# A preact convolution on one core: a regular pattern of combined images, all sums on the scalar engine, and a new order of its and the Pool's work

## The chip, the cores and the metric

The kernel runs on one core of a Trainium2 chip. The metric is the device time in microseconds (us) of one execution. The engines are PE (matmuls), PEld (its weight loads), DVE (vector), ACT (scalar), POOL (GpSimd) and SP (sync, which issues loads and stores).

## The reference

160 images of 128 channels and 32x32 pixels. Each gets a group norm (32 groups of 4 channels), then a 3x3 convolution with one of five weight sets, quantised in two steps, and is added to its input.

```python
x, U: (160, 128, 32, 32), (5, 128*128*9)      # both float32
s1 = (U.max() - U.min()) / 3;  v1 = s1 * floor(U / s1)
s2 = s1 / 5;                   v2 = s2 * floor((U - v1) / s2)
w  = (v1 + v2).reshape(640, 128, 3, 3)
y  = conv2d(group_norm(x, groups=32, eps=1e-5).reshape(32, 640, 32, 32),
            w, padding=1, groups=5)
return x + y.reshape(x.shape)
```

## The kernel before

The matmuls run in fp16. To keep the precision, the normalised image is split into a high part (a cast to fp16) and a low part (the difference). Pairs of rows share products: sums and differences of neighbouring rows go into a pair tile `m`, the rest goes directly into `eo`, and `m` is added to `eo` in between. There are two kinds of image from image 14 on:

- A **direct** image D: ACT makes `z` (normalised, f32) and casts it to `hi`; DVE makes `lo = z - hi` and the row combinations of `lo` alone. PE uses plain taps on `hi` and combinations of `lo`.
- A **combined** image C: the row differences and sums are taken of the raw image in f32 (`v`), ACT scales and casts them (`vh`), DVE makes the low part (`vl`). PE needs fewer matmuls. The first and the last row of the differences touch the padding; these two rows of 32 values are made by the Pool.

```python
STEADY = 14                      # images 14 to 155 may be combined
COMBINED = (1, 4, 6)             # residues modulo 8 of the combined images
MEASURED = (1, 5)                # residues measured by DVE, the others by ACT

def combine(self, i):
    v = self.v[i] = self.wide.tile([P, 2048], F32, ...)
    nc.gpsimd.tensor_scalar(v[:, :W], x[:, W:2*W], minus, -1.0, ALU.add, ALU.mult)
    nc.gpsimd.tensor_scalar(v[:, last:H*W], x[:, last-W:last], minus, 1.0, ALU.add, ALU.mult)
    nc.vector.tensor_sub(v[:, W:last], x[:, :last-W], x[:, 2*W:])
    # ... and two more DVE instructions for the sums and differences of pairs
```

One iteration of the main loop, cut to its order. Each engine works off its own instructions in this program order. `measure(k, (0,))` is the sum over an image and `(1,)` the sum of squares about the mean, each one ACT pass; `residual` evacuates `eo` to `sum`; `accumulate` has the Pool issue the DMA that adds `sum` to the image; `leave` copies half of `m` out of the matmul memory; `pairs` adds `m` to `eo` on DVE. The matmuls, `conv(i)`, come first: the pair sums of image i+1, then the rest of image i.

```python
self.residual(j); self.accumulate(j)                       # ACT, POOL
if self.combined(i + 1): measure stage 0                   # ACT
self.leave(i + 1)                                          # ACT
if not self.combined(i + 1): measure stage 0               # ACT
if self.combined(i + 3): self.high_combined(i + 3)         # ACT: vh
else:                    self.normalise(i + 3)             # ACT: z
measure stage 1                                            # ACT
if not self.combined(i + 3): self.high_part(i + 3)         # ACT: hi
# ... every 8 images: deviation, scales, deviations        # ACT, POOL
# ... 12 times: keep_column (a column of new weights)      # ACT, POOL
low_combined(i + 2)  or  low_part(i + 2)                   # DVE: vl / lo
take(later, 1)                                             # DVE: weight step
combinations(i + 2)  if direct                             # DVE
self.pairs(i + 1)                                          # DVE
if self.combined(i + 4): self.combine(i + 4)               # POOL rows, DVE
# ... images of residues 1 and 5 measured on DVE
```

## Time and profile before

| before | |
|---|---|
| time, median of 3 runs | 1057.66 us (1057.18 to 1061.2) |
| span in the profile | 1054.1 us |
| busy: PE, DVE, ACT, POOL | 94, 86, 80, 34% |
| combined images (`vh`) | 53 |
| images measured on DVE | 38 |

The prediction below shows the lines of the page, the waits and the chain.

A second measure is my own count from the trace and is called **lost** below: the time from each matmul's start to the next one's, less the median of that distance for its shape, summed over all distances that are more than 0.1 us too long.

### The profile page before, as it was taken

Reading aid. Unit: us, or ns where it says so; the run is one execution under the profiler, and the core shown is the slowest. Engines: PE = TensorE matmul, PEld = TensorE weight load, DVE = VectorE, ACT = ScalarE, POOL = GpSimd, SP = SyncE. Lnnn points to the kernel's source line nnn. Section 1 sums busy time; section 2 is a strip of 40 time slices with the busy share of each in tenths; the row PEclk is TensorE's granted clock in tenths of the full one; section 3 lists DMA queues with packets and bytes.
Section 4 is the critical chain, followed back from the end, with each engine's and each line's share of the span. In section 5 each row is a group of like instructions: output and inputs, shape, how many; then the busy total and the mean of one; then the engine's idle time right before and its main releaser. Section 6 shows DMA issues by size and latency. Waiting matters only on the chain.

```text
span 1054.1 us, 15898 instructions
## 1 busy us (share of the span) xinstructions
PE 990.0 (94%) x5910; PEld 574.7 (55%) x5910; DVE 909.0 (86%) x1387; ACT 845.4 (80%) x1145; POOL 363.4 (34%) x519
## 2 busy tenths in 40 slices
PE   1889999999999999999999999999999999999997
PEld 0335555555555555555556565555555655555554
DVE  7978898988999999889999988898998888888763
ACT  4889888888888887878888888888887888887660
POOL 3514244343425152523343333415161613233310
PEclk9999999999999999999999999999999999999999
DMA  9537989999999989899899999999989899987763
GB/s 364 209 100 219 247 235 248 249 248 265 264 258 251 260 235 270 234 277 269 231 276 240 264 245 254 276 254 249 261 242 247 231 265 261 266 236 182 175 174 125
DMA packets 67287, 254.42 MB, mean 241 GB/s; under 512 B 5248, under 2 KB 5248, under 8 KB 67200
## 3 DMA queue, kind: packets, MB, share of 16 engines
q1 hardware_dynamic: 45168, 173.09, 48.1%
q0 software_dynamic: 22032, 80.23, 39.6%
q8 instruction: 48, 0.79, 0.3%
q14 instruction: 39, 0.32, 0.1%
HBM read 89.19 MB, written 83.89 MB: 164 GB/s over the span
## 4 chain that ended last, share of the span: by engine, by line
PE 69%; DVE 21%; ACT 6%; issue 3%; DMA 1%; POOL 0%; SPq 0%; DVEq 0%; ACTq 0%
PE eo L608 32%; PE m L634 20%; PE eo L634 15%; DVE lo L568 4%; DVE eo L697 2%; DVE rows L582 2%; DVE eo L696 2%; ACT junk L192 2%; ACT z L511 2%; DVE v L544 2%; ACT hi L519 1%; DVE rows L584 1%; DVE rows L585 1%; DVE v L547 1%; DVE v L550 1%
## 5 line engine op out<-in xcount | busy, mean ns | idle before, releaser
L634 PEld LDWEIGHTS <-wt 128*128 128x128 f16 x3780 | 367.8, 98 | 255.5 <-DVE eo L697 36.8
L608 PE MATMUL eo<-hi,wt 128*128 128x496 f16 (+1 forms) x1908 | 458.7, 377 | 1.1 <-ACT wt L476 1.1
L724 POOL DMA_DIRECT2D xt<-sum x153 | 134.8, 881 | 478.1 <-ACT sum L711 473.2
L608 PEld LDWEIGHTS <-wt 128*128 128x128 f16 x1980 | 194.6, 100 | 186.5 <-issue 4.2
L711 ACT ACTIVATE sum<-eo 128x1024 f32<-128x1024 f32 x153 | 156.2, 1021 | 97.1 <-PE eo L634 88.4
L634 PE MATMUL eo<-rows,wt 128*128 128x248 f16 (+1 forms) x1248 | 187.9, 273 | 0.0
L634 PE MATMUL m<-rows,wt 128*128 128x496 f16 (+1 forms) x624 | 153.6, 383 | 27.9 <-DVE eo L697 27.8
L568 DVE TENSOR_TENSOR lo<-z,hi 128x1024 f16<-128x1024 f32 x107 | 130.9, 1224 | 55.3 <-ACT hi L519 55.3
L561 DVE SCALAR_TENSOR_TENSOR vl<-v,rstd,vh 128x2048 f16<-128x2048 f32 x53 | 124.4, 2347 | 22.8 <-ACT vh L555 22.8
L199 ACT ACTIVATE junk<-xt,mv 128x1024 f16<-128x1024 f32 x122 | 139.2, 1141 | 0.3
L192 ACT ACTIVATE junk<-xt 128x1024 f16<-128x1024 f32 x122 | 129.4, 1061 | 11.5 <-DMA xt<-in_x_dram 11.3
L696 DVE TENSOR_TENSOR eo<-m,m 128x512 f32<-128x512 f32 x157 | 108.9, 693 | 29.0 <-ACT m L687 27.0
L511 ACT ACTIVATE z<-xt,shift,rstd 128x1024 f32<-128x1024 f32 x107 | 132.9, 1242 | 0.6 <-POOL shift L242 0.6
L687 ACT COPY m<-m 128x512 f32<-128x512 f32 x157 | 91.6, 584 | 49.6 <-PE m L634 49.6
L555 ACT ACTIVATE vh<-v,rstd 128x2048 f16<-128x2048 f32 x53 | 105.9, 1998 | 22.6 <-POOL v L541 20.0
L634 PE MATMUL eo<-vh,wt 128*128 128x248 f16 (+1 forms) x636 | 121.7, 273 | 0.0
L634 PE MATMUL eo<-vl,wt 128*128 128x248 f16 (+1 forms) x636 | 121.7, 273 | 0.0
L634 PE MATMUL m<-vh,wt 128*128 128x496 f16 (+1 forms) x318 | 120.8, 380 | 0.9 <-DVE eo L697 0.9
L634 PE MATMUL m<-vl,wt 128*128 128x496 f16 (+1 forms) x318 | 120.7, 380 | 0.0
L697 DVE TENSOR_TENSOR eo<-m,m 128x512 f32<-128x512 f32 x157 | 109.8, 700 | 5.4
L519 ACT CAST hi<-z 128x1024 f16<-128x1024 f32 x107 | 111.1, 1039 | 0.9
L582 DVE TENSOR_TENSOR rows<-lo 128x1024 f16<-128x1024 f16 x104 | 72.8, 700 | 1.3
(109 smaller groups left out, 825.5 us busy)
## 6 DMA issues: line engine op xcount, KB each, us to landing
xt<-in_x_dram SPq DMA_DIRECT2D x78, 1024.0 KB, 9.6
out_dram<-xt SPq DMA_DIRECT2D x78, 1024.0 KB, 5.7
xt<-sum POOLq DMA_DIRECT2D x153, 512.0 KB, 7.2
range<-in_L_conv_U_dram SPq DMA_DIRECT2D x4, 576.0 KB, 7.4
u<-in_L_conv_U_dram SPq DMA_DIRECT2D x4, 576.0 KB, 11.8
xt<-in_x_dram SPq DMA_DIRECT2D x4, 512.0 KB, 10.3
out_dram<-xt SPq DMA_DIRECT2D x3, 512.0 KB, 2.9
u<-in_L_conv_U_dram SPq DMA_DIRECT2D x2, 288.0 KB, 3.1
```

What stands on the lines that cost most here:

```text
L192: self.nc.scalar.activation(junk, image, ACTF.Copy, scale=-1.0 / image.shape[1], accum_out=self.mv[:, j, 0:1],)
L199: self.nc.scalar.activation(junk, image, ACTF.Square, bias=self.mv[:, j, 0:1], accum_out=self.mv[:, j, 1:2],)
L511: nc.scalar.activation(z, self.image(i), ACTF.Identity, bias=st.shift[:, j : j + 1], scale=st.rstd[:, j : j + 1],)
L519: self.nc.scalar.copy(hi.rearrange("p h w -> p (h w)"), self.z[i])
L561: self.nc.vector.scalar_tensor_tensor(vl, self.v[i], st.rstd[:, j], self.hi[i], ALU.mult, ALU.subtract)
L568: self.nc.vector.tensor_sub(lo[:, 1 : self.H + 1, :].rearrange("p h w -> p (h w)"), self.z.pop(i), self.hi[i].rearrange("p h w -> p (h w)"),)
L608: nc.tensor.matmul(target[:, h, r0 - h0 : r1 - h0, c0:c1], self.wts[n, col][:, k, :], tile[:, s0 : s0 + r1 - r0, c0 + dw : c1 + dw], start ...
L634: self.nc.tensor.matmul(target[:, :, c0:c1], self.wts[n, col][:, kind, :], source[:, :, c0 + dw : c1 + dw], start=start, stop=stop, skip_g ...
L696: nc.vector.tensor_add(rows[:, :, 0], m[:, 0], m2)
L697: nc.vector.tensor_sub(rows[:, :, 1], m[:, 0], m2)
L711: nc.scalar.mul(self.sum[i], eo, 0.5)
L724: self.nc.gpsimd.dma_start(self.image(i), self.sum.pop(i), accum_op=ALU.add)
```

## The change

It means to let PE run without a gap: fewer matmuls (every second image combined, in place of three of eight), in a regular alternation of C and D. DVE is relieved of its measuring to pay for this, ACT takes it over, and ACT's order is rearranged so that the sums run ahead of the evacuation, and `hi` directly behind `z`. The two rows on the Pool are issued right behind the accumulating DMA. The last image is finished one half (one bank of the matmul memory) at a time.

```diff
-    COMBINED = (1, 4, 6)
-    MEASURED = (1, 5)
+    COMBINED = (1, 3, 5, 7)
+    MEASURED = ()
@@
-    def combine(self, i):
+    def outer_rows(self, i):
         # ... the two gpsimd.tensor_scalar
+    def combine(self, i):
         # ... the three DVE instructions
@@ conv
+        for halves in ((0,), (1,)) if i == self.imgs - 1 else ((0, 1),):
+            for col in self.COLS:
+                if col != self.COLS[0]:
+                    on_the_way(col)
+                self.rest_of_column(i, col, halves)
@@ the loop, in its new order (start-up cases cut)
+            if self.combined(i + 2):
+                self.low_combined(i + 2)
+            if direct:
+                self.low_part(i + 2)
+            take(later, 1)
+            if direct:
+                self.combinations(i + 2)
+            for k in by_scalar:
+                self.measure(k, (0,))
             if i > self.FIRST and not self.by_hand(j):
                 self.residual(j)
                 self.accumulate(j)
+            if self.combined(i + 4):
+                self.outer_rows(i + 4)
             if self.FIRST < i + 1 < self.imgs:
                 self.leave(i + 1)
             if self.combined(i + 3):
                 self.high_combined(i + 3)
             elif self.FIRST < i + 3 < self.imgs:
                 self.normalise(i + 3)
+                self.high_part(i + 3)
             for k in by_scalar:
                 self.measure(k, (1,))
-            if part and not self.combined(i + 3):
-                self.high_part(i + 3)
             # ... deviation, scales, deviations, keep_column as before
             # ... pairs and combine as before
```

More of the change, by code (lines that the diff above doesn't have):

```diff
@@ L543, in combine @@
         )
+    def combine(self, i):
+        nc, H, W = self.nc, self.H, self.W
+        st, j = self.column_of(i)
+        v, x, last = self.v[i], self.image(i), (H - 1) * W
         nc.vector.tensor_sub(v[:, W:last], x[:, : last - W], x[:, 2 * W :])
@@ L592, in halves, with taps @@
         )
-    def taps(self, i, part, col, target, last):
+    def taps(self, i, part, col, target, last, halves=(0, 1)):
         nc, H, W = self.nc, self.H, self.W
@@ L602, in taps @@
         for k in (1, 0, 2):
-            for h in range(2):
+            for h in halves:
                 h0 = h * (H // 2)
@@ L664, in conv, with rest_of_column @@
             self.sums_of_pairs(i + 1)
-        eo = self.eo[i]
-        for col in self.COLS:
-            if col != self.COLS[0]:
-                on_the_way(col)
-            last = col == self.COLS[-1]
-            if not self.combined(i):
-                self.taps(i, (self.hi[i], 0), col, eo, False)
-            for a, kind in enumerate((0, self.MINUS_G2)):
-                both = self.both(i)
-                for j, (d, _) in enumerate(both):
-                    for h in range(2):
-                        rows = slice(h * 16 + a, h * 16 + 16, 2)
-                        to = eo[:, h].rearrange("p (i a) w -> p a i w", a=2)[:, a]
-                        self.product(
-                            to, i, kind, d[:, rows, :], col, False,
-                            last and a == 1 and j == len(both) - 1,
-                        )
-        del self.v[i]
+        for halves in ((0,), (1,)) if i == self.imgs - 1 else ((0, 1),):
[3 more added lines that the diff above has]
+                self.rest_of_column(i, col, halves)
+        del self.v[i]
+    def rest_of_column(self, i, col, halves):
+        eo, both = self.eo[i], self.both(i)
+        if not self.combined(i):
+            self.taps(i, (self.hi[i], 0), col, eo, False, halves)
+        for a, kind in enumerate((0, self.MINUS_G2)):
+            for j, (d, _) in enumerate(both):
+                for h in halves:
+                    rows = slice(h * 16 + a, h * 16 + 16, 2)
+                    to = eo[:, h].rearrange("p (i a) w -> p a i w", a=2)[:, a]
+                    self.product(
+                        to, i, kind, d[:, rows, :], col, False,
+                        col == self.COLS[-1] and a == 1 and j == len(both) - 1,
+                    )
     def leave(self, i):
@@ L887, in run @@
             by_scalar = [k for k in to_measure if not self.by_vector(k)]
-            if i != self.FIRST:
+            direct = self.FIRST < i + 2 < self.imgs and not self.combined(i + 2)
+            if i < self.FIRST:
+                self.residual(j)
+                if i == self.FIRST - 1:
+                    self.leave(i + 1)
+                    self.pairs(i + 1)
+            if self.combined(i + 2):
[5 more added lines that the diff above has]
+                self.combinations(i + 2)
+            if i > self.FIRST and self.by_hand(j):
+                self.residual(j)
+            for k in by_scalar:
+                self.measure(k, (0,))
+            if i > self.FIRST and not self.by_hand(j):
                 self.residual(j)
                 self.accumulate(j)
-            if self.combined(i + 1):
-                for k in by_scalar:
-                    self.measure(k, (0,))
-            if self.FIRST <= i + 1 < self.imgs:
+            if self.combined(i + 4):
+                self.outer_rows(i + 4)
+            if self.FIRST < i + 1 < self.imgs:
                 self.leave(i + 1)
-            if not self.combined(i + 1):
-                for k in by_scalar:
-                    self.measure(k, (0,))
-            part = self.FIRST < i + 3 < self.imgs
             if self.combined(i + 3):
                 self.high_combined(i + 3)
-            elif part:
+            elif self.FIRST < i + 3 < self.imgs:
                 self.normalise(i + 3)
+                self.high_part(i + 3)
             for k in by_scalar:
                 self.measure(k, (1,))
-            if part and not self.combined(i + 3):
-                self.high_part(i + 3)
             for st in middle:
@@ L917, in run @@
             turned = []
-            low = i + 2 if self.FIRST < i + 2 < self.imgs and not self.combined(i + 2) else None
-            if self.combined(i + 2):
-                self.low_combined(i + 2)
-            if low is not None:
-                self.low_part(low)
-            take(later, 1)
-            if low is not None:
-                self.combinations(low)
-            if self.FIRST <= i + 1 < self.imgs:
+            if self.FIRST < i + 1 < self.imgs:
                 self.pairs(i + 1)
```

## The prediction

> **What bounds the kernel now.** I read the page's first part, then the waits of PE, then the chain in one period of eight images (508.10 to 557.84 us), then the timeline of the scalar engine there.
>
> ```profile
> PE 990.0 (94%) x5910; PEld 574.7 (55%) x5910; DVE 909.0 (86%) x1387; ACT 845.4 (80%) x1145; POOL 363.4 (34%) x519
> ...
> q1 hardware_dynamic: 45168, 173.09, 48.1%
> q0 software_dynamic: 22032, 80.23, 39.6%
> ```
>
> PE is the fullest engine, but DVE, ACT and the DMA engines (48.1 + 39.6 = 88%) are not far behind. The waits of all engines hold this line for PE:
>
> ```profile
> PE m L634 <- DVE eo L697: 28.7, 21, 5.2
> ```
>
> One of the 21 is the 5.2 us at 59 to 65 us, where the first direct images end. The other 20, together 23.5 us, lie between 140 and 1000 us, mostly one or two in a period. PE then waits for the DVE to empty the one pair tile `m`. The chain shows what the matmuls cost:
>
> ```profile
> 508.10 1.30 PE m L634 x6
> 509.39 2.63 PE eo L634 x24
> ...
> 518.58 2.59 PE m L634 x12
> ...
> 545.00 1.27 PE eo L608 x6
> 546.27 0.44 PE eo L634 x4
> ```
>
> A direct image D is six pair sums (1.30) and three columns of 1.27 + 0.44, so 6.43 us. A combined image C is 2.59 + 2.63 = 5.22 us. The period holds 5 D and 3 C: 32.15 + 15.66 = 47.8, and 0.4 for the statistics' and weights' small matmuls, 48.2 us. It took 49.74. The rest is waiting, of which the largest piece, in the timeline, is
>
> ```profile
> 543.53 1.47 PE L634 MATMUL m<-rows,wt 128*128 128x512 f16 x6 [1.20 <-DVE eo L697]
> ```
>
> Followed back in the chain it is a run of DVE work without a gap from 532.80, which began late because the cast to `hi` on ACT was late: ACT had done its evacuation, sum, normalisation and second measuring pass first. So **PE bounds each stage, and a queue of ACT then DVE steals about 1.4 us a period from it**.
>
> ACT in order, from the same timeline:
>
> ```profile
> 510.96 1.99 ACT L555 ACTIVATE vh<-v,rstd 128x2048 f16<-128x2048 f32 x1
> 512.86 1.14 ACT L199 ACTIVATE junk<-xt,mv 128x1024 f16<-128x1024 f32 x1
> 513.99 1.00 ACT L711 ACTIVATE sum<-eo 128x1024 f32<-128x1024 f32 x1
> 514.89 0.57 ACT L687 COPY m<-m 128x512 f32<-128x512 f32 x1
> 515.36 1.07 ACT L192 ACTIVATE junk<-xt 128x1024 f16<-128x1024 f32 x1
> 516.41 1.24 ACT L511 ACTIVATE z<-xt,shift,rstd 128x1024 f32<-128x1024 f32 x1
> 517.54 1.14 ACT L199 ACTIVATE junk<-xt,mv 128x1024 f16<-128x1024 f32 x1
> 518.67 1.04 ACT L519 CAST hi<-z 128x1024 f16<-128x1024 f32 x1
> 519.61 0.16 ACT L217 COPY ngm<-pg 128x8 f32<-128x8 f32 x1
> ```
>
> The reader should take start to start, not the durations: vh 1.90, second measuring pass 1.13, evacuation 0.90, `m` copy 0.47, first pass 1.05, z 1.13, hi 0.94. Over the whole period the windows view gives
>
> ```profile
> 508.10:557.84 49.74, 48.54 (x296) 28.51 (x295) 46.02 (x72) 42.29 (x57) 18.28 (x26) 1.00 0.93 250
> ```
>
> (PE, weight loads, DVE, ACT, POOL, then clock, DMA share, GB/s).
>
> **What the Trainium skill says.** "TensorE: Matmul & The Clock Gate", Back-to-back issue gap, has an isolated gap of N/2.4 + 2.5 ns, 209 ns for 496 columns, and a sustained 131 ns for 512. The trace: six matmuls of 496 or 512 in 1.30 us, 217 ns; it agrees with the first, not with the second. So the saving is counted by columns. "Perfetto Trace Analysis", Optimizing Scalar/DVE Operations, says the acknowledgement half of a profiled instruction overlaps the next; the trace agrees (1.00 us shown, 0.90 to the next start). The same page, Identifying the Most-Contended Engine, warns that matmul occupancy does not measure the distance from the roofline; I use the PE sums above and the gaps, not the 94%. "DMA: Bandwidth & Descriptors", Issuing engines are not separate DMA queues, says all queues share the 16 DMA engines; the two shares above add to what the windows show (0.93).
>
> **The change part by part.**
>
> 1. *Every second image combined.* From image 14 to 155, residues 1, 4, 6 give 53 combined images (the groups show 53 vh), the odd ones give 71. 18 images go from 6.43 to 5.22: 18 x 1.21 = **21.8 us less PE work**, all on the bounding engine. On DVE one such image costs, start to start, 2.26 + 1.07 + 0.66 + 0.60 = 4.59 in place of 1.14 + 0.60 + 0.34 + 0.34 = 2.42; on ACT 1.90 in place of 2.07.
>
> 2. *All later images measured on ACT.* 38 images (76 half measurements in the groups) leave DVE, 1.69 us each, and cost ACT 1.05 + 1.13 = 2.18 each, 83 us. The period after (4 D, 4 C) is on PE 25.7 + 20.9 + 0.4 = **47.0**; on ACT 42.29 + 2 x 2.18 - 0.17 = **46.5**, of which about 0.9 is tails that overlap a wait, so some 45.6 of work; on DVE 46.02 - 3.4 + 2.2 - 0.5 (one step of weight work less) = **44.4**. PE remains the bound, by little.
>
> 3. *The order.* With D and C alternating I lay two iterations on PE's clock, starting at T with C's pair sums (2.59), then the eo part of a D (to 7.72), D's pair sums (1.30), the eo part of a C (to 11.65). ACT: the evacuation at T+2.1 (after a first measuring pass done early), `m` copy 3.0, vh 3.5 to 5.4, second pass, next first pass to 7.6, evacuation 7.7, `m` copy when the sums end at 9.05, z, hi to 11.6, second pass, first pass to 13.8, which is the next T+2.1. It closes, with 0.2 + 0.4 us spare in 11.65. DVE: combine to T+1.7, lo 2.8, combinations with one weight step 4.5, pairs of C to 5.9, weight step, vl to 8.6, weight step, pairs of D from 9.6 (the `m` copy) to 11.0. PE wants that `m` at 11.65: 0.6 us spare. So the cadence holds without a PE wait, and most of the 23.5 us should go as well. I leave 5 us for what repeats every eight or so images: the means and deviations, and a weight column (0.8 us of ACT, more than the pair's spare time, recovered over the next pairs). **18.5 us gained.** Without the new order, measuring last would put the `m` copy behind it, as now.
>
> 4. *Pool's two rows first.* vh waited 20.0 us in all for these rows (L541). Now they are issued right behind the accumulating DMA, before statistics: by the above they are done about 4 us before vh. This is part of the 0.2 us spare holding, not a sum of its own.
>
> 5. *The start.* ACT measures image 9 as well before the first `m` copy, 2.2 us, so I put that copy's end at 62.2 us (60.4 in the timeline of before). DVE then needs 1.33 for the pairs, 1.14 for lo and 1.28 for the combinations, and the first pair sums behind them start at 66.0 instead of 64.57: +1.5 us. Then, till image 11, ACT has 5.6 us of work in one iteration and 7.8 in the next, mean 6.7 against PE's 6.4 to 6.5; with the lead it has, about +1.2 us. Together **+2.7 us**.
>
> 6. *The last image bank by bank.* The same matmuls, but the first half's addition (0.6 us from start to start) and its store go under the second half's matmuls: **-0.6 us**.
>
> Sum: 1057.7 - 21.8 - 18.5 + 2.7 - 0.6 = 1019.5, say **1020 us**.
>
> **The rivals.**
> - *ACT becomes the bound.* For it: 46.5 of 47.0 us a period, and no spare for a late input. Against: the tails in that number, and the schedule closes. If each pair ran 0.4 us over, 71 pairs give +28 us: 1048, within 2% of before. If 0.15: 1030.
> - *The old wait only moves.* PE's wait for `m` stays at 1.4 us a period, since a C part leaves ACT and DVE just 3.9 us for `m` copy and pairs. For it: that is where today's wait stands. Then only the matmuls count: 1057.7 - 21.8 + 2 = 1038, just inside 2%.
> - *The DMA engines.* Share 0.93 to 0.95 in the periods. Scaled to 47/49.7 it is about 1.0, so loads or accumulations may come late. Against: in the period the share includes stretched packets, slices at 380 to 419 GB/s occur there with a mean of 252, and only startup has a visible wait of a measuring pass for a load (11.3 us). Loads land some 17 us before their first reader. If it bound, about 1035.
>
> **Range and chances.** The best case, no waits left and no loss at the start, is about 1012; all of the old waits kept is 1038. I take 1009 to 1038. The 2% mark is 1036.5, so most of the range is beyond it: faster 0.91, same 0.08, slower 0.01.
>
> **What would show it.** Right: combined pair sums and vh x71, no batch statistics on DVE, x160 for both measuring passes; PE about 968 us busy; a period of 47.0 to 47.6; PE's wait for the pairs down from 28.7 to about 12 us, mostly before 120 us; ACT near 924 us (91%), DVE near 880. Wrong: a period of 49 us with PE waiting for the pairs on every C to D turn (the order), ACT without gaps and longer than PE (the bound), measuring passes waiting for loads (DMA), or the start losing over 5 us.

## More of the kernel before

One view is added here, since the whole document compares by it: the windows view of the stretch from 400 to 600 us. Its columns are the window, its length, then the busy time of PE, PEld, DVE, ACT and POOL with the number of instructions, the granted clock, the DMA share and GB/s.

```profile
400.00:600.00 200.00, 194.01 (x1180) 114.03 (x1178) 181.60 (x275) 168.05 (x226) 73.77 (x100) 1.00 0.96 256
```

PE is busy for 194 of 200 us, and the other engines have room.

In the steady part (140 to 960 us) before lost 29.1 us.

## The result, and the profile after

The kernel after took 1009.75 us, median of 4 fast runs (1009.02 to 1011.47), and its result is correct. Against before in the same rounds the ratio is 0.9536 (95% interval 0.9511 to 0.9561), so it is 4.6% faster. A ratio here always compares the fast runs of two kernels from the same rounds, so it is not quite the ratio of the medians quoted. Before's median was 1059.07 us in these rounds and 1060.2 to 1061.4 in later ones, which is why ratios are used.

From the page after, the busy line (busy us, share of the span, instructions):

```profile
PE 964.8 (96%) x5910; PEld 575.6 (57%) x5910; DVE 886.5 (88%) x1197; ACT 931.2 (92%) x1279; POOL 369.5 (37%) x555
```

From the windows view after, the same stretch as before:

```profile
400.00:600.00 200.00, 200.00 (x1256) 121.71 (x1254) 188.71 (x251) 197.94 (x271) 79.19 (x117) 1.00 1.00 271
```

PE has no idle time left, and ACT is close behind with 197.94 us. The DMA share is 1.00. From the waits view after, PE's waits (total us, times, longest us):

```profile
PE m L640 <- DVE rows L590: 7.3, 1, 7.3
...
PE m L640 <- DVE eo L706: 2.2, 5, 0.6
```

The first line is the start: the first pair sums wait 7.3 us where they waited 5.2, which are part of the 28.7 us of before. The other 23.5 us are down to 2.2, all of them before 140 us. Over the steady part the lost time went from 29.1 us to 0.0. The chain after shows the alternation (start, us, what), with the pieces of one D between two C:

```profile
507.40 2.59 PE m L640 x12
509.99 1.27 PE eo L614 x6
...
515.12 1.30 PE m L640 x6
516.41 2.63 PE eo L640 x24
519.04 2.59 PE m L640 x12
```

Two images take 519.04 - 507.40 = 11.64 us, the 11.65 of the prediction. The piece durations are those of before to 0.01 us.

**Where the time went.** The span fell from 1054.1 to 1007.8, by 46.3 us:

| | us |
|---|---|
| 18 images combined in place of direct, 1.21 each | -21.8 |
| lost time in the steady part, 29.1 to 0.0 | -29.1 |
| lost time before 140 us, 19.4 to 24.4 | +5.0 |
| after the last matmul, 7.12 to 7.01 | -0.1 |
| first matmul 0.6 us earlier, the rest not assigned | -0.3 |

The table stands for the two profiled runs, and before's, 1055.82 us at a mean granted clock of 0.995, is the fastest of before. In the next rounds before took 1056.2 us at 0.995, 1058.9 and 1060.2 at 0.992, and 1060.3 to 1062.1 at 0.989. So the gain by the medians, 49.3 us, is 3 us more than the table has. That fits further short spells at half clock behind PE's waits, of which the profiled run has one in the steady part (see below), but the unprofiled runs cannot show it.

### The profile page after: what moved, and what is told of

It reads as the page before. It is cut to its first block, busy times and chain, and to the rows that moved or that the text cites. A ratio compares the mean times of both kernels' runs of the same rounds, so it can differ in the third digit from the quotient of the medians.

```text
span 1007.8 us, 15892 instructions
## 1 busy us (share of the span) xinstructions
PE 964.8 (96%) x5910; PEld 575.6 (57%) x5910; DVE 886.5 (88%) x1197; ACT 931.2 (92%) x1279; POOL 369.5 (37%) x555
## 4 chain that ended last, share of the span: by engine, by line
PE 88%; ACT 7%; issue 2%; DVE 1%; POOL 1%; DMA 1%; SPq 0%
PE eo L614 30%; PE eo L640 28%; PE m L640 28%; ACT junk L199 2%; ACT z L511 1%; ACT junk L192 1%; ACT hi L519 1%; ACT sum L720 1%; DMA range<-in_L_conv_U_dram 1%; DVE ext L422 1%; DVE ext L423 1%; ACT m L696 0%; PE pg L225 0%; PE m L614 0%; PE pg L208 0%
## 5 line engine op out<-in xcount | busy, mean ns | idle before, releaser
L614 PE MATMUL eo<-hi,wt 128*128 128x496 f16 (+3 forms) x1584 | 381.8, 377 | 1.1 <-ACT wt L476 1.1
L199 ACT ACTIVATE junk<-xt,mv 128x1024 f16<-128x1024 f32 x160 | 183.3, 1146 | 0.4
L192 ACT ACTIVATE junk<-xt 128x1024 f16<-128x1024 f32 x160 | 169.1, 1057 | 14.1 <-DMA xt<-in_x_dram 10.7
L567 DVE SCALAR_TENSOR_TENSOR vl<-v,rstd,vh 128x2048 f16<-128x2048 f32 x71 | 166.7, 2348 | 3.5 <-ACT vh L561 3.5
L640 PE MATMUL eo<-vl,wt 128*128 128x248 f16 (+1 forms) x852 | 162.9, 273 | 0.0
L640 PE MATMUL eo<-vh,wt 128*128 128x248 f16 (+1 forms) x852 | 162.9, 273 | 0.0
L640 PE MATMUL m<-vh,wt 128*128 128x496 f16 (+1 forms) x426 | 161.8, 380 | 0.0
L640 PE MATMUL m<-vl,wt 128*128 128x496 f16 (+1 forms) x426 | 161.7, 380 | 0.0
L640 PE MATMUL m<-rows,wt 128*128 128x512 f16 x516 | 127.0, 383 | 9.5 <-DVE rows L590 7.3
L550 DVE TENSOR_TENSOR v<-xt 128x960 f32<-128x960 f32 x71 | 81.7, 1150 | 0.0
```

The lines of the kernel that those rows point to most:

```text
L192: self.nc.scalar.activation(junk, image, ACTF.Copy, scale=-1.0 / image.shape[1], accum_out=self.mv[:, j, 0:1],)
L199: self.nc.scalar.activation(junk, image, ACTF.Square, bias=self.mv[:, j, 0:1], accum_out=self.mv[:, j, 1:2],)
L567: self.nc.vector.scalar_tensor_tensor(vl, self.v[i], st.rstd[:, j], self.hi[i], ALU.mult, ALU.subtract)
L614: nc.tensor.matmul(target[:, h, r0 - h0 : r1 - h0, c0:c1], self.wts[n, col][:, k, :], tile[:, s0 : s0 + r1 - r0, c0 + dw : c1 + dw], start ...
L640: self.nc.tensor.matmul(target[:, :, c0:c1], self.wts[n, col][:, kind, :], source[:, :, c0 + dw : c1 + dw], start=start, stop=stop, skip_g ...
```

## The experiments

The question was what removed the lost 29 us: the counts, ACT's order, or the Pool's rows. Medians are of 4 fast runs (5 for the last two), the lost time is that of the one profiled run; all results were correct. "Before, same rounds" was 1060.2 to 1061.4 throughout.

### The counts alone, in the old order

```diff
-    COMBINED = (1, 4, 6)
+    COMBINED = (1, 3, 5, 7)          # combined_only
-    MEASURED = (1, 5)
+    MEASURED = ()                    # both_old_order has this as well
```

> The kernel before with only the odd images combined (71), measuring and order as before. Theory A (the new order is what removed PE's waits): 21.8 us less matmul work, but the waits of PE for the pairs stay near 1.4 us a period, and DVE has 46.0 + 2.2 - 0.5 = 47.7 us of work a period against PE's 47.0, so about 1037 us. Rival B (the regular C-D alternation removes the waits, whatever the order): bound by DVE at 47.8 a period, about 1020 us.

> The kernel before with the odd images combined and all images measured on ACT, order as before. Theory A: the matmul saving alone, PE still waits some 20 us or more for the pairs between 140 and 960 us, about 1037 us or slower. Rival B (alternation, with DVE relieved of measuring, removes the waits): as the changed kernel, 1010 to 1014 us.

`combined_only` took 1038.13 us, ratio 0.9794 (0.9767 to 0.9821), and lost 30.3 us: the matmul saving of 21.8 came alone, and none of the lost time. This is the 1038 that the prediction's second rival named. `both_old_order` took 1049.48, ratio 0.9907 (0.9878 to 0.9936), and lost 37.3 us. Taking the measuring from DVE made it **worse** by 11 us, 7 of them in the steady part and nearly 4 before 140 us. Its waits view, limited to 140 to 960 us, says what ACT waits for:

```profile
ACT vh L555 <- POOL v L541: 44.3, 25, 3.4
```

The Pool's second row comes late for 25 of the combined images, by up to 3.4 us. In before that line has 20.0 us, 15 times, longest 1.6.

### The order alone, and the order without the measuring

```diff
-    COMBINED = (1, 3, 5, 7)
+    COMBINED = (1, 4, 6)             # order_only (of after)
-    MEASURED = ()
+    MEASURED = (1, 5)                # order_only and new_order_vector
```

> The changed kernel with combined residues 1, 4, 6 and measuring of 1, 5 on DVE as before: the order alone. Theory A: PE's waits between 140 and 960 us fall from some 29 us lost to under 8, so about 1035 us. Rival B: the waits stay because the irregular sequence C D C D D stays, about 1056 us.

> The changed kernel, but residues 1 and 5 are measured on DVE as before. If DVE's work matters (47.7 us a period against PE's 47.0): waits of PE for the pairs come back, about 0.7 to 1.5 us a period, 1020 to 1035 us. If ACT, which has no idle time in the changed kernel, is the one that matters: 1005 to 1010 us.

`order_only` took 1035.85, ratio 0.9777 (0.9749 to 0.9805), and lost 9.6 us. `new_order_vector` took 1024.26, ratio 0.9662 (0.9635 to 0.9689), and lost 18.1. In the latter DVE is nearly full, as its window from 400 to 600 us shows (third busy time):

```profile
400.00:600.00 200.00, 196.06 (x1218) 116.95 (x1217) 195.50 (x282) 176.42 (x231) 84.45 (x111) 1.00 0.98 264
```

The table has the medians of the six combinations:

| | counts of before | odd images, DVE measures | odd images, ACT measures |
|---|---|---|---|
| old order | 1060.3 | 1038.1 | 1049.5 |
| new order | 1035.9 | 1024.3 | 1009.75 |

The counts of combined images and the order each gain on their own. It is the measuring that needs the order: moving it to ACT costs 11 us in the old order and gains 14.5 in the new one.

### Which part of the order: the Pool's rows or the sums

One part of after is undone at a time.

```diff
 # rows_late
-            if self.combined(i + 4):
-                self.outer_rows(i + 4)             # right behind accumulate
@@
             if self.combined(i + 4):
+                self.outer_rows(i + 4)             # back, after the statistics
                 self.combine(i + 4)
 # sums_late
-            for k in by_scalar:
-                self.measure(k, (0,))              # ahead of residual
             self.residual(j); self.accumulate(j)
+            if self.combined(i + 1): measure stage 0     # the old places
             ...
             self.leave(i + 1)
+            if not self.combined(i + 1): measure stage 0
```

> The changed kernel with Pool's two rows issued where they were, behind the statistics and the weight column in Pool's queue. Theory P (with both counts changed it was Pool's rows that held vh, hence vl and PE: in the run with the old order ACT waited 44.3 us for them): most of the 36 us of that run come back, 1030 to 1048 us, and ACT waits over 30 us for L541's counterpart. Theory S (measuring sums ahead of the evacuation is what matters): little changes, 1010 to 1015 us.

> The changed kernel with the first measuring pass back in its old places, behind the evacuation or the m copy. Theory P: 1009 to 1014 us. Theory S: the m copy and the pairs come about 1 us later in every other iteration, where the schedule on paper has 0.6 us to spare, so 0.4 us a pair of images and 71 pairs: 1030 to 1040 us.

`rows_late` took 1053.02, ratio 0.9938 (0.9917 to 0.9959), and lost 41.5 us. **Two instructions of 32 columns, issued later, give back 43 us**, nearly the whole gain; the time lies beyond the 1030 to 1048 us that was expected. `sums_late` took 1012.99, ratio 0.9546 (0.9527 to 0.9566), and lost 0.8 us; 3.2 us by the medians, though the intervals of the ratios overlap with after's.

How two rows can cost so much is seen in the Pool's timeline. The columns are start, duration, engine, line and operation, and in brackets the idle time before it and what ended that. First `rows_late`, in an iteration with statistics and a weight column:

```profile
531.08 1.81 POOL L235 TENSOR_TENSOR rstd<-ve,mhalf 128x8 f32<-128x8 f32 x1 [2.42 <-ACT ve L231]
532.99 0.86 POOL L239 TENSOR_SCALAR rstd<-rstd,lift 128x8 f32<-128x8 f32 x1
...
535.77 0.92 POOL L481 TENSOR_SCALAR wt<-wt 128x128 f16<-128x128 f16 x1
...
536.94 0.28 POOL L540 TENSOR_SCALAR v<-xt,ngm 128x32 f32<-128x32 f32 x1
```

The row takes 0.28 us, but it stands in the queue behind eight instructions that begin at 531.08 and waits for `ve` of ACT with them. It could have run before: DVE's timeline has its own part of the same tile `v` begin at 528.94, from the same image. ACT's timeline of `rows_late` then has

```profile
537.26 2.00 ACT L561 ACTIVATE vh<-v,rstd 128x2048 f16<-128x2048 f32 x1 [3.09 <-POOL v L540]
```

DVE's `vl` follows, and then `pairs`; PE's timeline ends the story with the next pair sums:

```profile
544.48 0.39 PE L640 MATMUL m<-vh,wt 128*128 128x512 f16 x1 [2.97 <-DVE eo L706]
```

3.09 us late on ACT has become 2.97 on PE: with three engines this full, nothing on the way absorbs it. Between 140 and 960 us ACT waits 42.8 us for this row, 25 times, against 41.5 lost on PE. Now after, in the corresponding iteration:

```profile
505.24 0.90 POOL L733 DMA_DIRECT2D xt<-sum  x1 [0.31 <-ACT m L696]
505.91 0.57 POOL L539 TENSOR_SCALAR v<-xt,ngm 128x32 f32<-128x32 f32 x1
506.18 1.56 POOL L540 TENSOR_SCALAR v<-xt,ngm 128x32 f32<-128x32 f32 x1
508.59 1.84 POOL L235 TENSOR_TENSOR rstd<-ve,mhalf 128x8 f32<-128x8 f32 x1 [0.85 <-ACT ve L231]
```

The row is done at 507.74, ahead of the statistics, though by itself it took 1.56 us here. ACT reaches `vh` at 511.56 without a wait, and in the waits view after, from 140 to 960 us, no line has ACT waiting for the Pool's rows. The Trainium skill, "Perfetto Trace Analysis", section Tensor Engine Instruction (MATMUL, LD_WEIGHTS), says that the queues of ACT, DVE and GpSimd are strict FIFO; these traces agree, as the 0.28 us row, ready by 528.94, is not let past.

### The rows alone, added to the old order

For this the DVE's low block has to stand ahead of the rows in program order, so it is moved along.

```diff
             self.residual(j); self.accumulate(j)
+            ... low_combined / low_part, take(later, 1), combinations   # moved up
+            if self.combined(i + 4):
+                self.outer_rows(i + 4)
             ... the rest in the old order
```

`both_rows_first` is this on `both_old_order`; `before_rows_first` is this on before.

> The kernel before with odd images combined, all measured on ACT, and Pool's two rows issued right behind the accumulating DMA, ACT's order as before. Theory P: the large waits go, 1010 to 1022 us. Theory S: as the run with the old order, 1040 to 1050 us.

> The kernel before with one thing moved: Pool's two rows are issued right behind the accumulating DMA. Counts, measuring and ACT's order as before. Theory P: the 29 us that PE lost between 140 and 960 us were mostly these rows too (ACT waited 20.0 us for them), so 1037 to 1043 us. Theory S (there the late cast to hi, an ACT order matter, made the waits): 1052 to 1058 us.

`both_rows_first` took 1013.31, ratio 0.9564 (0.9545 to 0.9584), and lost 2.1 us: the rows alone give 36 us there and leave 3.6 to after. So with the new counts the rest of ACT's order, sums first and `hi` behind `z`, is worth a few us.

`before_rows_first` took 1060.86, ratio 0.9997 (0.9973 to 1.0022): nothing, and this is a miss of the theory that late rows are what costs time in general. The small gain that the other theory allowed, to 1052 to 1058 us, did not come either. It lost 32.6 us (29.1 in before; its steady part has three spells at half clock where before's has one). The rows did come in time, since the 20.0 us wait for them is gone from the waits view; PE's wait stayed, 23.7 us in place of 23.5. The waits point to another one with the old counts: DVE's for the cast `hi`. The three views below hold this line of the waits view from 140 to 960 us, of before, `before_rows_first` and `order_only` in turn:

```profile
DVE lo L568 <- ACT hi L519: 39.5, 32, 2.8
```

```profile
DVE lo L573 <- ACT hi L519: 39.8, 32, 2.8
```

```profile
DVE lo L574 <- ACT hi L519: 5.2, 9, 0.8
```

In `order_only`, which has ACT's new order beside the early rows, PE's wait for the pairs falls from 23.5 to 6.6 us, so with the old counts ACT's order has to change. Whether it would do without the early rows, and whether the sums ahead of the evacuation or the `hi` directly behind `z` did it, was not run and stays open. The total of a wait does not tell its cost: `both_rows_first` still has 27.8 us on this line, 58 times, and PE lost 2.1.

### The start

```diff
-    MEASURED = ()
+    MEASURED = (9, 13)
-        return i >= self.EARLY and i % 8 in self.MEASURED
+        return i in self.MEASURED       # DVE measures these two images only
```

> The changed kernel, but images 9 and 13 are measured on DVE as before; nothing else. The start lost 4.9 us of PE time up to 140 us against before (5 us of waits); if these two measurements on ACT are the cause, 1005 to 1007 us, and the first wait for the pair sums is 5 us again instead of 7.3. If the order at the start is the cause, 1009.5 us.

`start_vector` took 1007.67, ratio 0.95 (0.9483 to 0.9517), about 2 us less than after by the medians; the intervals of the ratios just touch. Lost time before 140 us fell from 24.4 to 21.3, and the first wait for the pair sums from 7.3 to

```profile
PE m L640 <- DVE rows L590: 4.8, 1, 4.8
```

so ACT's extra measuring at the start is 3 of the 5 us that the start lost. 1007.67 is just outside the expected 1005 to 1007.

### Is the DMA share of 1.00 a bound?

```diff
+            if i >= 14:
+                extra = self.spare.tile([P, 256], F32, tag="extra", name=f"extra{i}")
+                nc.sync.dma_start(extra, self.xv[n, :, b, :256])   # 128 KB nobody reads
```

> The changed kernel with 128 KB more loaded for every image from 14 on, into a buffer nobody reads. The DMA share of the windows is 1.00 in the changed kernel. If that share means that the DMA engines are full, the added quarter of a load, some 0.3 us of all 16 engines by the rate of a load, comes on top: 146 x 0.3 = +44 us, 1054 us. If it doesn't, as the load's lead of 11 to 16 us before its first reader suggests, 1009 to 1013 us.

`more_dma` took 1023.26 (1019.54 to 1028.81), ratio 0.9653 (0.9617 to 0.969), and lost 10.9 us in the steady part. It moved 290 GB/s from 400 to 600 us, where after moved 271:

```profile
400.00:600.00 200.00, 198.53 (x1244) 120.48 (x1243) 186.60 (x248) 196.44 (x268) 74.86 (x112) 1.00 1.03 290
```

Neither answer fits: had the engines been full, it would have lost some 44 us; had they had room, nothing. It lost 13.5. A new line in the waits of DVE says through what:

```profile
DVE nn L99 <- DMA u<-in_L_conv_U_dram: 11.4, 3, 6.8
```

Three loads of new weights, of 576 KB each, came late, one of them by 6.8 us; behind that one alone PE lost 7.7 of the 10.9 us, 5.3 waiting and 2.4 at half clock. The same line after, from the start to the end, is

```profile
DVE nn L99 <- DMA u<-in_L_conv_U_dram: 1.0, 2, 0.6
```

So two of the three weight loads of the steady part had no lead left in after (in before they landed 2.3, 1.0 and 1.7 us ahead of their reader). PE lost nothing by it: the share of 1.00 doesn't bind there, but the margin is used up. The loads of images had more: by my count from the trace they landed 14 us ahead of their first reader in the median after (18 in before, 12 here, between 140 and 850 us). The experiment is not quite clean, since the extra loads also make SP wait for their two buffers (61.1 us, 21 times). For the worst load that is not the main thing: it was issued 10.8 us before DVE came to it, where after had 12.1, and took 17.6 us to land, where after's took 11.2.

### Better versions

`best_a` is `start_vector` with two output buffers for the unread results of the measuring passes, and with the last image's `eo` in two tiles in place of one. `best_b` has `STEADY = 9` besides, which combines images 9, 11 and 13 too.

```diff
-        self.unread = pool("unread", 1)
+        self.unread = pool("unread", 2)
@@ pairs, last image
+            first = self.ps_eo.tile(shape, F32, tag="eo", ...)
+            second = self.ps_tr.tile(shape, F32, tag="pt", ...)
```

> The changed kernel with images 9 and 13 measured on DVE, two buffers for the unread output of the measuring passes (one buffer makes a second pass wait 0.16 us for the first), and the last image's two banks as two tiles, so that the first half's addition waits for its own matmuls only. Expected: 1007.7 of the first of these alone, minus 0.6 at the end, minus 0.5 to 1.5 in the first 140 us where ACT is behind: 1005 to 1007 us.

> As the last one, with images 9, 11 and 13 combined as well: 3 x 1.21 us less matmul work and 0.17 us less ACT work each, 1001.5 to 1004 us; if the start is held by ACT or DVE rather than PE, nothing is gained and it is 1005 to 1007 us.

`best_a` took 1004.51, ratio 0.9467 (0.9451 to 0.9482); `best_b` 1003.19, ratio 0.9455 (0.9439 to 0.9471). Both are faster than after, and are not to be told apart from each other. The three images of `best_b` save 3.6 us of matmuls by the prediction's figure, but its trace lost 21.0 us before 140 us and 2.2 after, which is 3.9 more than that of `best_a`. `best_a` lost 19.35 us before 140 us, which is before's 19.4: the start's whole loss is recovered, though what the second buffer did of this was not measured alone.

The last image shows why bank by bank gave after nothing. DVE's timeline, after:

```profile
1000.85 1.29 DVE L725 SCALAR_TENSOR_TENSOR xt<-eo,xt 128x512 f32<-128x512 f32 x2 [3.90 <-PE eo L640]
```

Both halves' additions (x2) run together, after PE's last matmul at 1000.81: the first half waited for the end of all matmuls into its tile. With two tiles, in `best_a`:

```profile
993.58 0.69 DVE L749 SCALAR_TENSOR_TENSOR xt<-eo,xt 128x512 f32<-128x512 f32 x1 [1.34 <-PE eo L651]
996.14 0.69 DVE L749 SCALAR_TENSOR_TENSOR xt<-ep,xt 128x512 f32<-128x512 f32 x1 [1.87 <-PE ep L651]
```

The first half goes 2.6 us ahead, and the time from PE's end to the end of the span is 6.59 us in place of 7.01.

## Why the prediction was right, and where its steps were not

The direction and the range were right: 1009.75 against 1020, only 0.75 us above the low edge of 1009 to 1038, and even beyond the "best case" of 1012. That the range still held is partly luck. Of the sizes below, two were off by 10.6 us and by 2.3, in opposite directions.

1. **The matmul saving, 21.8 us: right.** `combined_only` isolates it: its lost time is about that of before (30.3 against 29.1), and it gained 22 us.
2. **The loads of the engines: right.** Busy PE 964.8 (968 predicted), ACT 931.2 (924), DVE 886.5 (880; the prediction's sum for DVE's period is 44.3 and not 44.4); eight images take 46.84 us (507.40 to 554.24 in the chain) against 47.0.
3. **The order, 18.5 us: too small, 29.1.** Two terms were mis-sized. The 23.5 us of waits is idle time after the *modelled* end of the last matmul; by spacing, the same 20 waits cost 26.8, some 0.16 us more each; six more of 0.10 to 0.15, which show no idle time, cost 0.7; and after one of the 20 PE ran at half clock for a while, another 1.6. That makes 29.1. And the 5 us reserve for statistics and weight columns was not needed: PE lost nothing to them in the steady part.
4. **The Pool's rows, "not a sum of its own": wrong.** This is the step that failed. The prediction saw the 20.0 us wait in the profile, and counted it as one small condition among those for the spare 0.2 us. `rows_late` loses 43 us without it and `both_rows_first` gains 36 by it alone. The prediction had checked that the rows would be early in the new place, which was true ("about 4 us before vh"; 3.8 in the iteration above), but not what they would do in the old one under the new counts: 5.6 us of statistics and weight work ahead of them in the queue, and no slack behind. Also the sentence that without the new order the `m` copy would stay behind the measuring "as now" named the wrong cause: with the new counts and the rows early, `both_rows_first` keeps ACT's old order and is 3.6 us behind after, `sums_late` 3.2.
5. **The start, +2.7 us: too small, +5.0.** The first pair sums began at 65.86, where 66.0 was predicted (64.57 before). But PE came to them 0.8 us earlier than before, so its wait grew by 2.1. The larger miss is what follows: 3.2 us of waits between 100 and 140 us, where before has 0.3 and 1.2 more was predicted. A spell at half clock at 30 us, 1.1 longer after, and a wait of 1.1 at 39 us that only before has cancel. On the clock the Trainium skill, "TensorE: Matmul & The Clock Gate", section What's actually happening, names half clock after an idle window of about 3.4 us; here it also followed a gap of only 2.1 us before 793.91 in the trace of before (clock 0.5 from 795.0 to 798.4), though not the gaps of 2.0 to 2.2 us before 194.59, 394.28 and 594.07.
6. **The last image, -0.6 us: wrong, about 0**, since the halves shared a tile; `best_a` with two has 0.4.
7. **A reading of the DMA shares.** The prediction adds 48.1 and 39.6% and finds the windows' 0.93 in them. The sum is 88%, of the whole span. In a stretch like the windows' (500 to 550 us) the two queues have 49.9 and 44.0%, and these do add to 0.94.

The rivals. "ACT becomes the bound" fell, but by little: 197.94 of 200 us with PE at 200.00. "The old wait only moves" is exactly `combined_only` and not after. "The DMA engines" fell for after, where the late weight loads cost PE nothing, but with no margin left, as `more_dma` shows.

What is shown is that the Pool's place in the queue decides with the new counts, by undoing it and by doing it alone. What decides within ACT's order with the old counts stays open.

## What to carry to other kernels

A tiny instruction on an idle engine (37% busy here) can hold the whole kernel if it stands in an in-order queue behind others that wait: place it where its inputs are ready, and ask of each wait in the profile what it would cost once the slack around it is gone. A change can be harmful alone and pay together with another (measuring on ACT: 11 us worse in the old order, 14.5 better in the new), so test them in combination. To finish a result in parts, give each part a tile of its own, as a wait on a shared one lasts until its last writer.

## What the Trainium skill lacked or had wrong

- "TensorE: Matmul & The Clock Gate", Back-to-back issue gap: the sustained gap of 131 ns for 512 columns was not seen; matmuls of 496 and of 512 columns followed each other at 216 ns in the median (12 in 2.59 us). So the isolated gap that the prediction quotes beside it fits 512 columns, but not 496, for which it gives 209. Rows of 31 values took as long as rows of 32 (465 columns 203 ns, as 480; 248 columns 110, and 256 109).
- The same page, What's actually happening: half clock was seen after a shorter gap than its window of about 3.4 us, 2.1 us of idle time before 793.91 us in before, at a cost of 1.6 us, and not after three others of that size.
- "Perfetto Trace Analysis", Identifying the Most-Contended Engine, calls DMA occupancy misleading. The runs agree (share 1.00 and no PE time lost; 7% more traffic cost 13.5 us), but no page says how to read the margin left; the lead of the weight loads over their first reader served here (1.0 to 2.3 us in before, none for two of three after, 6.8 us late in `more_dma`).
- "GPSIMD Engine Reference" gives dispatch and per-element costs of large operations, no duration for the tiny ones here: a power of 128x8 values took 1.74 us in the mean in before, and a row of 128x32 between 0.28 and 2.83 us (median 0.59 for the second row), as the profile shows them.
- No page has the rate of a DMA of the Pool that accumulates into a tile: its 4 KB packets took 328 ns in the median in before, plain ones of 4 KB 159 ns.
